# Inverse square roots of 160 norms: a power on GpSimd in place of nine VectorE passes

## The chip, the cores and the metric

The kernel runs on one core of one Trainium2 chip. A core has five engines that each work through their own list of instructions in order and wait for each other by semaphores: TensorE (matrix products; PE in the profile, and PEld for its loads of weights), VectorE (DVE), ScalarE (ACT), GpSimd (POOL) and SyncE (SP, which here only issues DMAs). TensorE writes its results to PSUM; the other data lie in SBUF, over 128 partitions. The metric is the device time of one execution in microseconds (us), as the median of several runs.

## The reference

Eight residual layers are applied in a row to a float32 tensor `x` of shape (2, 1024, 256): two batches of 1024 tokens of 256 channels.

```python
x = x + L0_attn_a(layernorm(x))    # softcapped attention, 16 heads
x = x + L0_ffn(layernorm(x))       # 256 -> 512 -> 512 -> 256, relu
x = x + L0_attn_b(layernorm(x))    # causal attention, 16 heads of 16
x = x + L0_ffn(layernorm(x))
x = x + L1_attn_a(layernorm(x))    # difference of two softmaxes, softmax again, rms norm
x = x + L1_ffn(layernorm(x))       # gated, 256 -> 2048 -> 256, 4-bit weights
x = x + L1_attn_b(layernorm(x))    # a linear model that learns along the tokens
x = x + L1_ffn(layernorm(x))
```

Inverse square roots of a sum plus a small constant appear in three places: in every `layernorm` (eps 1e-5), in the rms norm of each head in `L1_attn_a`, and three times in `L1_attn_b`: keys are divided by their length, the outputs are normalised twice, and the recurrent step itself has one:

```python
def step(S, inp):                                # 64 steps of 16 tokens each
    qi, ki, vi, ei = inp
    kh = einsum('bchd,bhde->bche', ki, S)
    mu = mean(kh, -1); rstd = rsqrt(var(kh, -1) + 1e-6)
    kh_hat = (kh - mu) * rstd
    g = w * kh_hat + b - (vi - ki); gw = g * w
    v_new = (gw - mean(gw) - kh_hat * mean(gw * kh_hat)) * rstd
    ...
    S = S - einsum('bchd,bche->bhde', ki * ei, v_new)
```

Each step needs the `S` of the step before. (The kernel prepares its data so that the mean of `kh` need not be taken off.)

## The kernel before, in words

`x` stays in SBUF as 16 tiles of 128 tokens (`self.x`). The work runs in five functions, with the feed-forward layers woven between the attention work: `attn_a_ffn0` (0 to some 445 us in the profile), `attn_b` (to some 876 us), `ffn0_dequantize` (to 1024 us; it also unpacks the 4-bit weights), `attn_d_ffn1` (to some 2100 us) and `ttt_ffn1` (the linear model and the last feed-forward layer, to the end).

The order of the work is written by hand. `in_order()` (line 372) makes PE, DVE, ACT and POOL execute their instructions in the order in which the Python code emits them; nothing is moved later. Each function cuts its work into small steps and emits them by due times: in `attn_d_ffn1` by the table `SCHED`, in `ttt_ffn1` by the table `TTT`. A round of the linear model is one of the 64 recurrent steps. It emits the tokens `K Q k q d 0 1 s 2 3` in this order, and a step of other work whose due time is `n + m` goes into round `n` at the fraction `m` of that list. `0` is `squares`, `1` is `root`, `s` updates the state, `2` is `gradient`, `3` is `finish` (lines 1984 to 2013). One tile of 128 tokens in both batches is eight rounds.

`rsqrt` (line 260) is called 160 times. It computes `1/sqrt(scale * x + add)` on VectorE in nine instructions (lines 269 to 279): `n` is the scaled sum, the integer form of `n` times -0.5 plus a constant is a first guess, and seven more passes refine it. Its result is the inverse root with a **minus sign**, and the callers are written for that. The calls:

- `layernorm_apply` (line 294), 64 calls, of 128 partitions x 2 columns. `layernorm_stats` finds mean and variance on VectorE and turns the sign of the mean on GpSimd (line 291); `layernorm_apply` takes the inverse root and then normalises the two tiles on GpSimd (line 300). `layernorm_turn` (or `turn` in `ffn0_pieces`) transposes them on TensorE (lines 315, 521) and copies them with a factor -1.
- `root` of a linear-model step (line 1989), 64 calls of 128 x 4. ScalarE squares `kh`, VectorE sums (line 1987), takes the inverse root, and multiplies (`hat`, line 1992).
- `normalize` of the keys (line 1805), 8 calls of 128 x 32, with one more pass that turns the sign (line 1808), and `root` of the outputs (line 2048), 16 calls of 128 x 32: the first (`step` 0) right after its sum (line 2046), the second (`step` 1) one due time later.
- `root` in `attn_d_out` (line 1406), 8 calls of 128 x 32; `normalize` (line 1416) uses the result, for the first three tiles at once, for later tiles about a round later.

GpSimd's other work in `attn_d_ffn1` is `rescale` (lines 1307 to 1315) and `lower` (line 1331), both inside the chain of each pair of heads; in `ttt_ffn1` it has `by_w` (line 1818), `halves` (line 1858, which waits for a DMA) and `gate` (lines 2056, 2059).

Of the kernel before, what the change touches and what calls it, by code (L numbers as in the profile page):

```python
# [10 lines left out]
F32 = mybir.dt.float32  # L11
I32 = mybir.dt.int32
BF16 = mybir.dt.bfloat16
AF = mybir.ActivationFunctionType
ALU = mybir.AluOpType
# [6 lines left out]
P = 128  # L22
# [117 lines left out]
class Net:  # L140
# [17 lines left out]
    def make_constants(self):  # L158
        nc, const = self.nc, self.const
        self.ident = const.tile([P, P], F32, name="ident")  # L160
        make_identity(nc, self.ident)

        self.neg = const.tile([P, P], F32, name="neg")
        nc.gpsimd.memset(self.neg, 0.0)
        nc.gpsimd.affine_select(
            out=self.neg, in_=self.neg, compare_op=ALU.is_ge, fill=NEG, base=0,
            pattern=[[-1, P]], channel_multiplier=1,
        )
        self.tri = const.tile([P, P], F32, name="tri")
        nc.gpsimd.memset(self.tri, 1.0)  # L170
        nc.gpsimd.affine_select(
            out=self.tri, in_=self.tri, compare_op=ALU.is_ge, fill=0.0, base=0,
            pattern=[[1, P]], channel_multiplier=-1,
        )

        self.ident_h, self.neg_h, self.negT_h = (
            const.tile([P, P], BF16, name=n) for n in ("ident_h", "neg_h", "negT_h")
        )
        nc.vector.tensor_copy(self.ident_h, self.ident)
        nc.vector.tensor_copy(self.neg_h, self.neg)  # L180
        nc.vector.tensor_scalar(
            self.negT_h, self.tri, 1.0, -NEG, ALU.subtract, ALU.mult
        )
        self.eps = {}
        for v in (1e-5, 1e-6, 1e-8):
            e = const.tile([P, 1], F32, name=f"eps{len(self.eps)}")
            nc.gpsimd.memset(e, v)
            self.eps[v] = e
        self.minus12 = const.tile([P, 1], F32, name="minus12")
        nc.gpsimd.memset(self.minus12, -12.0)  # L190

# [67 lines left out]

    def rsqrt(self, work, x, scale, add, tag):  # L260

        nc = self.nc
        y, z, w, n = (
            work.tile(list(x.shape), F32, tag=f"{tag}_{k}", name=f"rsq_{k}") for k in "yzwn"
        )
        k = (1024.0 / 27.0) ** 2
        nc.vector.tensor_scalar(n, x, k * scale, k * add, ALU.mult, ALU.add)
        nc.vector.tensor_scalar(  # L270
            y.bitcast(I32), n.bitcast(I32), -0.5, 1597463007.0, ALU.mult, ALU.add
        )
        nc.vector.tensor_tensor(z, y, y, ALU.mult)
        nc.vector.tensor_tensor(w, z, n, ALU.mult)
        nc.vector.scalar_tensor_tensor(z, w, -10.0 / 3.0, w, ALU.add, ALU.mult)
        nc.vector.scalar_tensor_tensor(y, z, 5.0, y, ALU.add, ALU.mult)
        nc.vector.tensor_tensor(z, y, y, ALU.mult)
        nc.vector.tensor_tensor(w, z, n, ALU.mult)
        nc.vector.scalar_tensor_tensor(y, w, -64.0 / 3.0, y, ALU.add, ALU.mult)  # L279
        return y  # L280

    def layernorm_stats(self, work, tiles):
# [26 lines left out]
    def layernorm_turn(self, work, pt, xn, by_parity, on_vector=False, bufs=2):  # L309

        nc = self.nc
        for b in range(B):
            for kc in range(2):
                src = xn[:, b, kc::2] if by_parity else xn[:, b, kc * P : (kc + 1) * P]
                nc.tensor.transpose(pt[:, kc, b * P : (b + 1) * P], src, self.ident)
        xT = work.tile([P, 2, B * P], F32, tag="xT", name="xT", bufs=bufs)
        if on_vector:
            nc.vector.tensor_scalar_mul(xT, pt, -1.0)
        else:
            nc.scalar.activation(xT, pt, AF.Copy, scale=-1.0)  # L320
        return xT

    def project(self, out, xT, tt, w, lo, hi):
# [174 lines left out]
    def ffn0_pieces(self, work, bank, i, w1, w2, w3, b1, b2, b3, scalar=False):  # L498
# [16 lines left out]
        def turn(p):  # L515
            if p == 0:
                f.xT = work.tile([P, 2, 512], F32, tag="fx", name="fxT", bufs=1 + scalar)
            pt = bank("ln_t").rearrange("p (k t) -> p k t", k=2)
            for j in range(2):
                for kc in range(2):  # L520
                    nc.tensor.transpose(
                        pt[:, kc, j * P : (j + 1) * P], f.xn[p][:, j, kc * P : (kc + 1) * P],
                        self.ident,
                    )
            xT = f.xT[:, :, 2 * p * P : 2 * (p + 1) * P]
            if scalar:
                nc.scalar.activation(xT, pt, AF.Copy, scale=-1.0)
            else:
                nc.vector.tensor_scalar_mul(xT, pt, -1.0)

        def hidden(m, part, src, w, bias, dst):
            n = w.shape[1]
# [863 lines left out]
    def attn_d_out(self, ps, work, tile_, wo, i):  # L1396


        nc = self.nc

        def squares():
            flat = tile_.turned.rearrange("p b t n d -> p (b t n) d")
            tile_.sq = work.tile([P, 32, 16], F32, tag="pair", name="sq", bufs=1)
            nc.gpsimd.tensor_tensor(tile_.sq, flat[:, :, 0:16], flat[:, :, 0:16], ALU.mult)

        def root():
            flat = tile_.turned.rearrange("p b t n d -> p (b t n) d")
            r, s2 = (work.tile([P, 32], F32, tag=k, name=k) for k in ("r", "s2"))
            nc.vector.tensor_reduce(r, tile_.sq, AX.X, ALU.add)
            nc.vector.scalar_tensor_tensor(  # L1410
                s2, flat[:, :, 16], 16e-8, flat[:, :, 16], ALU.mult, ALU.mult
            )
            nc.vector.tensor_tensor(r, r, s2, ALU.add)
            tile_.r = self.rsqrt(work, r, 1.0 / 16.0, 0.0, "or")

        def normalize():
            pair = work.tile([P, 4, 4, 32], F32, tag="pair", name="pair", bufs=1)
            by_pair = tile_.turned.rearrange("p b (u t) n d -> p (b u) t n d", t=2)
            rt = tile_.r.rearrange("p (i t n) -> p i t n", t=2, n=4)
            for t in range(2):  # L1420
                nc.vector.tensor_tensor(
                    pair[:, :, :, 16 * t : 16 * t + 16], by_pair[:, :, t, :, 0:16],
                    rt[:, :, t, :].unsqueeze(3).to_broadcast([P, 4, 4, 16]), ALU.mult,
                )
            tile_.yT = work.tile([P, 4, P], F32, tag="yT", name="yT", bufs=1)
            nc.vector.transpose(
                tile_.yT.rearrange("p i q -> p (i q)"), pair.rearrange("p i n d -> p (i n d)")
            )

        def project():  # L1430
            po = self.bank(ps, "po").rearrange("p (b c) -> p b c", b=B)
            for b in range(B):
                for u in range(2):
                    nc.tensor.matmul(
                        po[:, b], tile_.yT[:, 2 * b + u, :], wo[:, u, :],
                        start=(u == 0), stop=(u == 1),
                    )

                xs = self.x[:, b * NB + i, :]
                nc.vector.tensor_tensor(xs, xs, po[:, b], ALU.subtract)  # L1440

        return squares, root, normalize, project

# [113 lines left out]
    def ttt_ffn1(self, w, deq):  # L1557
# [11 lines left out]
        with ExitStack() as ctx:  # L1569
# [33 lines left out]

            t.w2 = big.tile([P, 4, D], F32, name="w2")
            for b in range(B):
                nc.vector.scalar_tensor_tensor(
                    t.w2[:, 2 * b : 2 * b + 2, :], w["ln_w_hc"], -1.0, w["ln_w_hc"],
                    ALU.mult, ALU.mult,
                )

            t.ones = big.tile([1, P], F32, name="ones")
# [3 lines left out]
            for kc in range(2):  # L1615
                wv = w["wqkv"][:, kc, 512:768]
                nc.vector.scalar_tensor_tensor(wv, wv, -1.0, w["ln_w"], ALU.mult, ALU.mult)

                nc.vector.tensor_scalar(
                    w["wo"][:, kc, :], w["wo"][:, kc, :], w["norm_w"][:, kc : kc + 1], -1.0,  # L1620
                    ALU.mult, ALU.mult,
                )
            t.w_out = big.tile([P, C], F32, name="w_out")
            nc.vector.tensor_scalar_mul(t.w_out, w["ln_w"], -1.0)
            t.S = big.tile([P, 4, D], F32, name="S0")
            nc.vector.memset(t.S, 0.0)
            ctx.enter_context(self.in_order())
# [103 lines left out]
    def ttt_inputs(self, i):  # L1731
# [73 lines left out]
        def normalize():  # L1805
            t_.uk = work.tile([P, B, 8, 2, 2, D], F32, tag="uk", name="uk", bufs=1)
            rk = self.rsqrt(work, t_.rk, 1.0, 1e-6, "rk")
            nc.vector.tensor_scalar_mul(rk, rk, -1.0)
            kn = t_.uk[:, :, :, :, 1, :].rearrange("p b h f d -> p (b h f) d")
            nc.vector.tensor_tensor(  # L1810
                kn, t_.k.rearrange("p b (h d) -> p (b h) d", d=D),
# [113 lines left out]
        def own_rates():  # L1925
# [7 lines left out]
            nc.vector.tensor_reduce(  # L1933
                eta.rearrange("p n (b f) -> p f b n", f=2), own, AX.X, ALU.add
            )
            nc.vector.tensor_scalar_add(eta, eta, 1.0)

        def gates():
            sg = t_.sg = work.tile([P, B, C], F32, tag="sg", name="sg")
# [16 lines left out]
    def ttt_step(self, n, data, last):  # L1956
# [25 lines left out]
                )  # L1982

        def squares():
            sq, own.sm = tile_("k_sq"), tile_("var", (P, 4))
            nc.scalar.activation(sq, own.kh, AF.Square)
            nc.vector.tensor_reduce(own.sm, sq, AX.X, ALU.add)

        def root():
            own.rstd = self.rsqrt(work, own.sm, 1.0 / D, 1e-6, "kr")  # L1990
            own.hat = tile_("hat")
            nc.vector.tensor_tensor(own.hat, own.kh, by_g(own.rstd), ALU.mult)

# [23 lines left out]
    def ttt_outputs(self, i, data):  # L2017
# [36 lines left out]
        def gate():  # L2054
            o = data.o
            nc.gpsimd.tensor_tensor(
                o, o, t.w_out.unsqueeze(1).to_broadcast([P, B, C]), ALU.mult
            )
            nc.gpsimd.tensor_tensor(o, o, data.q, ALU.add)

# [240 lines left out]
```

## Time and profile before

| what | value |
|---|---|
| median of 3 runs | 2863.79 us (2859.41 to 2870.02) |
| span of the profiled execution | 2865.0 us, 66910 instructions |
| mean granted TensorE clock | 0.932 |
| ScalarE busy | 1330.0 us (46%) |
| GpSimd busy | 1063.2 us (37%) |
| nine lines of `rsqrt`, VectorE busy in all | 284 us in 1440 instructions |

The profile has one time for the profiled execution, its span: from the first to the last instruction. It lies 1.2 us above the median of the timed runs, inside their range. A line of groups reads: line of the kernel, engine, operation, output <- input by tile names, shapes, count | busy time in all, mean ns of one | idle time of the engine just before them and what ended it. A line of the time view reads: start, duration, engine, line, operation, tiles, count, and in brackets how long the engine had been idle and what it waited for.

### The profile page before, as it was taken

What the parts mean: (1) busy time and instruction counts of PE and PEld (TensorE: products, weight loads), DVE (VectorE), ACT (ScalarE), POOL (GpSimd) and SP (SyncE); (2) the same over time, 40 slices, a digit from 0 to 9 for tenths busy, and PEclk for the clock granted to TensorE, in tenths of its full rate; (3) what the DMA queues carried; (4) which work ended last, traced back from release to release, by engine and by line L of the source; (5) the groups of instructions that cost most, each with busy time, mean ns of one, the idle gap of its engine ahead of it and who ended that gap; (6) DMA issues with size and microseconds to landing.
All of it is one profiled execution on the core that took longest, in us unless ns stands there. A gap on an engine that the chain in (4) does not pass through costs nothing.

```text
span 2865.0 us, 66910 instructions
## 1 busy us (share of the span) xinstructions
PE 2520.3 (88%) x26384; PEld 1555.7 (54%) x26384; DVE 2028.8 (71%) x6762; ACT 1330.0 (46%) x2800; POOL 1063.2 (37%) x1600
## 2 busy tenths in 40 slices
PE   6999998999998877988888888888868999989888
PEld 2334334444433444655655555555646777767777
DVE  5777774766767968679786878788656767767651
ACT  2686870345454435676666675757611222212110
POOL 3444242211115757567554665565510001101000
PEclk9999998999999966999998999899978999999898
DMA  4000000000001100000000000000011110101100
GB/s 122 1 1 1 1 1 1 1 1 1 1 1 45 45 1 1 1 1 1 1 1 1 1 1 1 1 1 1 1 35 25 25 25 22 21 15 35 25 9 15
DMA packets 61978, 35.37 MB, mean 12 GB/s; under 512 B 43216, under 2 KB 58080, under 8 KB 61664
## 3 DMA queue, kind: packets, MB, share of 16 engines
q1 hardware_dynamic: 59472, 29.49, 4.0%
q8 instruction: 207, 3.39, 0.5%
q10 hardware_dynamic: 2192, 1.61, 0.2%
q14 instruction: 107, 0.88, 0.1%
HBM read 22.68 MB, written 8.39 MB: 11 GB/s over the span
## 4 chain that ended last, share of the span: by engine, by line
PE 38%; DVE 14%; POOL 4%; ACT 4%; issue 3%; SPq 1%; DMA 1%; ACTq 0%; POOLq 0%; DVEq 0%
PE ph L1521 6%; PE pg L2115 5%; PE e L1273 4%; DVE p L1284 4%; PE pu L2115 4%; PE po L2133 3%; PE dT L1345 3%; PE po L1540 2%; DVE p L1323 2%; POOL p L1331 1%; PE py L1375 1%; POOL p L1311 1%; ACT p L1294 1%; PE kh L1726 1%; PE pq L327 1%
## 5 line engine op out<-in xcount | busy, mean ns | idle before, releaser
L1294 ACT ACTIVATE p<-p,nm 128x128 f32<-128x128 f32 (+7 forms) x512 | 391.2, 769 | 79.8 <-DVE nm L1290 42.2
L1284 DVE CUSTOM_DVE_ANT_0 p<-e,mask 128x512 f32<-128x512 f32 (+3 forms) x768 | 382.3, 553 | 61.4 <-PE e L1273 61.0
L1331 POOL TENSOR_SCALAR p<-p,md 128x128 f32<-128x128 f32 (+7 forms) x256 | 241.6, 948 | 180.0 <-DVE md L1323 162.6
L1359 ACT ACTIVATE pT<-dT 128x384 f32<-128x384 f32 (+3 forms) x384 | 176.6, 487 | 203.2 <-PE dT L1345 202.2
L1273 PE MATMUL e<-kT,qT 32*128 32x512 f32 (+3 forms) x1536 | 230.5, 580 | 43.7 <-DVE nm L1284 40.8
L1345 PE MATMUL dT<-ident,p 128*128 128x128 f32 x1152 | 197.1, 297 | 65.2 <-POOL p L1331 36.6
L1323 DVE CUSTOM_DVE_ANT_0 p<-p,nrs 128x128 f32<-128x128 f32 (+7 forms) x256 | 221.3, 890 | 25.9 <-POOL p L1315 25.7
L938 ACT ACTIVATE pr<-s 128x512 f32<-128x512 f32 (+3 forms) x384 | 157.3, 496 | 162.9 <-PE s L933 154.2
L1311 POOL TENSOR_SCALAR p<-p,ra,neg_lam 128x128 f32<-128x128 f32 (+7 forms) x256 | 219.5, 857 | 9.2
L1345 PEld LDWEIGHTS dT<-ident,p 128*128 128x128 f32 x1152 | 138.0, 149 | 153.5 <-POOL p L1331 67.9
L654 ACT ACTIVATE pr<-s 128x1024 f32<-128x1024 f32 (+1 forms) x192 | 145.4, 813 | 125.6 <-PE s L648 77.4
L2115 PE MATMUL pg<-xT,gate 128*128 128x256 f32 x576 | 158.6, 423 | 4.6 <-ACT inter L2120 3.4
L898 PE MATMUL s<-kT,qT 32*128 32x512 f32 (+3 forms) x768 | 155.0, 518 | 4.3 <-DVE q_pad L906 2.5
L906 DVE CUSTOM_DVE_ANT_0 masked<-s,mask 128x128 f32<-128x128 f32 (+3 forms) x256 | 110.7, 487 | 59.1 <-PE s L898 59.0
L659 ACT ACTIVATE pr<-pr 128x1024 f32<-128x1024 f32 (+1 forms) x192 | 152.2, 852 | 0.0
L2133 PE MATMUL po<-down,inter 128*128 128x256 f32 x576 | 144.2, 395 | 5.8 <-DVE inter L2125 5.8
L1273 PEld LDWEIGHTS e<-kT,qT 32*128 32x128 f32 x1536 | 84.8, 203 | 116.3 <-DVE nm L1284 72.7
L662 POOL TENSOR_SCALAR_AFFINE_SELECT pr<-pr 128x256 f32<-128x256 f32 x128 | 89.3, 716 | 152.1 <-ACT pr L659 55.1
L2115 PE MATMUL pu<-xT,up 128*128 128x256 f32 x576 | 141.3, 389 | 0.8 <-ACT inter L2120 0.7
L2120 ACT ACTIVATE inter<-pg 128x512 f32<-128x512 f32 x72 | 43.0, 597 | 195.7 <-PE pg L2115 195.7
L2115 PEld LDWEIGHTS pg<-xT,gate 128*128 128x128 f32 x576 | 116.5, 209 | 27.1 <-issue 4.7
L300 POOL TENSOR_SCALAR ln_xn<-x,ln_mv,rsq_y 128x256 f32<-128x256 f32 x128 | 89.8, 710 | 108.1 <-DVE rsq_y L279 88.8
(295 smaller groups left out, 5344.1 us busy)
## 6 DMA issues: line engine op xcount, KB each, us to landing
uk_d<-uk SPq DMA_DIRECT2D x128, 32.0 KB, 1.9
r<-uk_d SPq DMA_DIRECT2D x8, 512.0 KB, 3.5
x<-in_L_attn_a_X SPq DMA_DIRECT2D x4, 512.0 KB, 6.7
qh_d<-qh SPq DMA_DIRECT2D x8, 256.0 KB, 2.1
o<-qh_d SPq DMA_DIRECT2D x128, 16.0 KB, 1.8
out<-x SPq DMA_DIRECT2D x4, 512.0 KB, 4.4
w<-in_L_ffn_W2T SPq DMA_DIRECT2D x1, 1024.0 KB, 7.7
pk<-in_L_ffn_gate_packed SPq DMA_DIRECT2D x8, 128.0 KB, 2.4
```

The costliest lines, as they stand in the source:

```text
L938: nc.scalar.activation(pr[:, g, off:512], tiles[g][:, 0:m], AF.Exp, scale=0.25)
L1273: nc.tensor.matmul(own.tiles[h][:, a, 0 : hi - lo], made["q"][r : r + 32, a, t, :], kT[r : r + 32, a, lo:hi], start=True, stop=True,)
L1284: nc.vector.tensor_tensor_reduce(own.p[h][a][:, lo:hi], own.tiles[h][:, a, 0 : hi - lo], neg_row[:, T - nk + lo : T - nk + hi], -1.0, 3e38 ...
L1294: nc.scalar.activation(own.p[h][a], own.p[h][a], AF.Exp, bias=own.nm[:, h, a : a + 1], scale=-1.0, accum_out=own.sm[:, h, a : a + 1],)
L1311: nc.gpsimd.tensor_scalar(p1, p1, own.ra[:, h : h + 1], nlam[:, head : head + 1], ALU.mult, ALU.mult)
L1323: nc.vector.tensor_tensor_reduce(p0, p0, p1, own.nrs[:, h : h + 1], 3e38, ALU.add, ALU.min, own.md[:, h : h + 1],)
L1331: nc.gpsimd.tensor_scalar(p0, p0, -1.0, own.md[:, h : h + 1], ALU.mult, ALU.add)
L1345: nc.tensor.transpose(dT[:, n, :], own.p[h][0][:, kb * P : (kb + 1) * P], self.ident)
L1359: nc.scalar.activation(shared[t, s + h][:, lo:hi, :], own.dT[h, part][:, 0 : hi - lo, :], AF.Exp)
L1521: nc.tensor.matmul(ph[:, j, :], w[:, kc, m * P : (m + 1) * P], f.xT[:, kc, :], start=(kc == 0), stop=(kc == 1),)
L2115: nc.tensor.matmul(ph[:, j, :], m_[:, kc, m * P : (m + 1) * P], f.xT[:, kc, :], start=(kc == 0), stop=(kc == 1),)
L2133: nc.tensor.matmul(f.po[:, b], inter[m // 2][:, m % 2, b * P : (b + 1) * P], wd[:, m % 2, (m // 2) * C : (m // 2 + 1) * C], start=(b == m ...
```

## The change

`rsqrt` becomes one or two GpSimd instructions. If a scale is given, the first computes `scale * x + add`; the second raises that to the power -0.5, the exponent being a constant column that is read for every element. The result is positive now, so every caller's sign changes: copies lose their factor -1, two products lose theirs, the pass of line 1808 and the tile `w_out` go, and `eta` gets a factor -1 in the instruction that adds its constant.

In the recurrent step both numbers of the first instruction are moved elsewhere: ScalarE squares with scale `D ** -0.5`, so that the sum is a mean, and the tile of the squares has a 17th column that is set to 1e-6 once and is summed along. There, `rsqrt` is a single GpSimd instruction.

```diff
+        self.root = const.tile([P, 1], F32, name="root")
+        nc.gpsimd.memset(self.root, -0.5)
...
     def rsqrt(self, work, x, scale, add, tag):
         nc = self.nc
-        y, z, w, n = (
-            work.tile(list(x.shape), F32, tag=f"{tag}_{k}", name=f"rsq_{k}") for k in "yzwn"
-        )
-        k = (1024.0 / 27.0) ** 2
-        nc.vector.tensor_scalar(n, x, k * scale, k * add, ALU.mult, ALU.add)
-        nc.vector.tensor_scalar(
-            y.bitcast(I32), n.bitcast(I32), -0.5, 1597463007.0, ALU.mult, ALU.add
-        )
-        nc.vector.tensor_tensor(z, y, y, ALU.mult)
-        nc.vector.tensor_tensor(w, z, n, ALU.mult)
-        nc.vector.scalar_tensor_tensor(z, w, -10.0 / 3.0, w, ALU.add, ALU.mult)
-        nc.vector.scalar_tensor_tensor(y, z, 5.0, y, ALU.add, ALU.mult)
-        nc.vector.tensor_tensor(z, y, y, ALU.mult)
-        nc.vector.tensor_tensor(w, z, n, ALU.mult)
-        nc.vector.scalar_tensor_tensor(y, w, -64.0 / 3.0, y, ALU.add, ALU.mult)
+        y = work.tile(list(x.shape), F32, tag=f"{tag}_y", name="rsq_y")
+        if scale is not None:
+            n = work.tile(list(x.shape), F32, tag=f"{tag}_n", name="rsq_n")
+            nc.gpsimd.tensor_scalar(n, x, scale, add, ALU.mult, ALU.add)
+            x = n
+        nc.gpsimd.tensor_tensor(y, x, self.root.to_broadcast(list(x.shape)), ALU.pow)
         return y
...
-            nc.vector.tensor_scalar_mul(xT, pt, -1.0)
+            nc.vector.tensor_copy(xT, pt)
         else:
-            nc.scalar.activation(xT, pt, AF.Copy, scale=-1.0)
+            nc.scalar.copy(xT, pt)
...
-                nc.vector.tensor_tensor(xs, xs, po[:, b], ALU.subtract)
+                nc.vector.tensor_tensor(xs, xs, po[:, b], ALU.add)
...
-            t.w_out = big.tile([P, C], F32, name="w_out")
-            nc.vector.tensor_scalar_mul(t.w_out, w["ln_w"], -1.0)
+            t.sq = [big.tile([P, 4, D + 1], F32, name=f"k_sq{j}") for j in range(2)]
+            for sq in t.sq:
+                nc.gpsimd.memset(sq, 1e-6)
...
             rk = self.rsqrt(work, t_.rk, 1.0, 1e-6, "rk")
-            nc.vector.tensor_scalar_mul(rk, rk, -1.0)
...
-            nc.vector.tensor_scalar_add(eta, eta, 1.0)
+            nc.vector.tensor_scalar(eta, eta, -1.0, -1.0, ALU.mult, ALU.add)
...
         def squares():
-            sq, own.sm = tile_("k_sq"), tile_("var", (P, 4))
-            nc.scalar.activation(sq, own.kh, AF.Square)
+            sq, own.sm = t.sq[n % 2], tile_("var", (P, 4))
+            nc.scalar.activation(sq[:, :, 0:D], own.kh, AF.Square, scale=D ** -0.5)
             nc.vector.tensor_reduce(own.sm, sq, AX.X, ALU.add)
 
         def root():
-            own.rstd = self.rsqrt(work, own.sm, 1.0 / D, 1e-6, "kr")
+            own.rstd = self.rsqrt(work, own.sm, None, None, "kr")
```

More of the change, by code (lines that the diff above doesn't have):

```diff
@@ L526, in turn @@
             if scalar:
-                nc.scalar.activation(xT, pt, AF.Copy, scale=-1.0)
+                nc.scalar.copy(xT, pt)
             else:
-                nc.vector.tensor_scalar_mul(xT, pt, -1.0)
+                nc.vector.tensor_copy(xT, pt)
         def hidden(m, part, src, w, bias, dst):
@@ L1605, in ttt_ffn1 @@
             for b in range(B):
-                nc.vector.scalar_tensor_tensor(
-                    t.w2[:, 2 * b : 2 * b + 2, :], w["ln_w_hc"], -1.0, w["ln_w_hc"],
-                    ALU.mult, ALU.mult,
+                nc.vector.tensor_tensor(
+                    t.w2[:, 2 * b : 2 * b + 2, :], w["ln_w_hc"], w["ln_w_hc"], ALU.mult
                 )
@@ L1617, in ttt_ffn1 @@
                 nc.vector.scalar_tensor_tensor(wv, wv, -1.0, w["ln_w"], ALU.mult, ALU.mult)
-                nc.vector.tensor_scalar(
-                    w["wo"][:, kc, :], w["wo"][:, kc, :], w["norm_w"][:, kc : kc + 1], -1.0,
-                    ALU.mult, ALU.mult,
-                )
-            t.w_out = big.tile([P, C], F32, name="w_out")
-            nc.vector.tensor_scalar_mul(t.w_out, w["ln_w"], -1.0)
+                nc.vector.tensor_scalar_mul(
+                    w["wo"][:, kc, :], w["wo"][:, kc, :], w["norm_w"][:, kc : kc + 1]
+                )
+            t.sq = [big.tile([P, 4, D + 1], F32, name=f"k_sq{j}") for j in range(2)]
+            for sq in t.sq:
+                nc.gpsimd.memset(sq, 1e-6)
             t.S = big.tile([P, 4, D], F32, name="S0")
@@ L2056, in gate @@
             nc.gpsimd.tensor_tensor(
-                o, o, t.w_out.unsqueeze(1).to_broadcast([P, B, C]), ALU.mult
+                o, o, t.w["ln_w"].unsqueeze(1).to_broadcast([P, B, C]), ALU.mult
             )
```

## The prediction

> **What bounds the kernel now.** I read the page's first two parts, then the waits around the tile that all inverse roots write, then the time view of one recurrent step and one layer norm, then TensorE's waits and the chain of waits by stage.
>
> ```profile
> span 2865.0 us, 66910 instructions
> ...
> PE 2520.3 (88%) x26384; PEld 1555.7 (54%) x26384; DVE 2028.8 (71%) x6762; ACT 1330.0 (46%) x2800; POOL 1063.2 (37%) x1600
> ...
> PE   6999998999998877988888888888868999989888
> ...
> DVE  5777774766767968679786878788656767767651
> ...
> POOL 3444242211115757567554665565510001101000
> ```
>
> TensorE bounds the whole: 88% busy, 345 us idle. So an edit on VectorE or GpSimd pays only where TensorE waits for it. Three regions differ. To 1020 us TensorE is full except where it waits for a layer norm. In the attention of 1100 to 2100 us it is 847 of 1000 us busy, and VectorE (782) and GpSimd (591) take turns in its chain. In the linear model (2126 to 2760 us) it is busy 578 of 634 us, and GpSimd is nearly empty (59 us).
>
> The waits around the inverse roots (us, times):
>
> ```profile
>   POOL ln_xn L300: 88.8, 46
> ...
>   PE ln_t L315: 43.2, 12
> ...
>   PE ln_t L521: 26.0, 9
> ```
>
> GpSimd already waits for the nine passes before it normalises, and TensorE waits for that. One layer norm at 880 us:
>
> ```profile
> 880.30 0.18 DVE L289 BATCH_NORM_AGGREGATE ln_mv<-ln_st 128x2 f32<-128x6 f32 x1
> ...
> 880.67 0.19 POOL L291 TENSOR_SCALAR ln_mv<-ln_mv 128x2 f32<-128x2 f32 x1 [7.91 <-DVE ln_mv L289]
> ...
> 882.43 1.10 POOL L300 TENSOR_SCALAR ln_xn<-x,ln_mv,rsq_y 128x256 f32<-128x256 f32 x2 [1.57 <-DVE rsq_y L279]
> ```
>
> The variance is there at 880.48; GpSimd starts its small operation 0.1 to 0.2 us later, and then idles 1.57 us for VectorE. From variance to use: 1.95 us.
>
> One recurrent step, and what TensorE waits for in the linear model (total, times, longest):
>
> ```profile
> 2405.47 0.22 DVE L1987 TENSOR_REDUCE var<-k_sq 128x4 f32<-128x64 f32 x1 [0.23 <-ACT k_sq L1986]
> ...
> 2405.73 0.17 DVE L269 TENSOR_SCALAR rsq_n<-var 128x4 f32<-128x4 f32 x1
> 2405.93 0.17 DVE L270 TENSOR_SCALAR rsq_y<-rsq_n 128x4 int32<-128x4 int32 x1
> ...
> 2407.32 0.16 DVE L279 SCALAR_TENSOR_TENSOR rsq_y<-rsq_w,rsq_y 128x4 f32<-128x4 f32 x1
> 2407.58 0.23 DVE L1992 TENSOR_TENSOR hat<-kh,rsq_y 128x64 f32<-128x64 f32 x1
> ```
>
> ```profile
> PE kh L1726 <- DVE vs L2013: 6.8, 13, 1.9
> PE po L2133 <- DVE inter L2125: 5.8, 3, 3.0
> PE pqk L327 <- ACT xT L320: 4.8, 7, 0.7
> ...
> PE kh L1726 <- DVE hat L1992: 3.2, 1, 3.2
> PE kh L1726 <- DVE S L1703: 3.1, 4, 2.0
> ```
>
> Sum to product take 1.89 us of nine dependent passes, one each 0.2 us. The waits that VectorE (or a norm, through xT) causes add up to 23.7 us; most of the other 32 us are "issue". That is the ceiling here, whatever VectorE gains.
>
> **The price of a power.** No row of the trace shows it. Low end: an ordinary small GpSimd operation, 0.19 us (the sign of the mean, 128x2) for 2 or 4 columns, 0.27 us for 32 (the sign row plus 32 columns of 2.5 ns, from 1272 ns for 512 columns of line 2056). High end: every column as dear as such a whole instruction, 0.19 us each after a start of 0.19: 0.57, 0.95 and 6.3 us for 2, 4 and 32 columns. Between them I take the row of the same function: VectorE needs nine passes; nine passes at GpSimd's 2.5 ns a column are 22 ns, and a general power is a logarithm, a product and an exponential, so three times that, 65 ns a column (an estimate): 0.32, 0.45 and 2.3 us. The hand-overs have rows: 0.1 us from VectorE to GpSimd (the mean's sign after its sum, three instances looked at) and 0.05 us back (VectorE's line 1323 after GpSimd's line 1315).
>
> The row of GpSimd's two-input multiply (1272 ns, line 2056) against VectorE's of the same size (692 ns, line 2052) is 1.84 to 1. The Trainium skill, GPSIMD Engine Reference, section Engine selection, speaks against the change with just this: elementwise work belongs on VectorE, GpSimd being about twice as slow. By it alone one power would still cost only two of the nine passes it replaces, and the time would be that of the low end, 2788. The same page, section Instruction dispatch, says that the first call of a freshly loaded GpSimd routine costs about 6 us more; no row here shows it, and by it the sum below would be 6 us higher, once.
>
> **Layer norms (64 calls).** Out: nine passes. In: two GpSimd operations behind the mean's sign, which ran beside the passes before and is now in series: 0.1 + 0.19 + 0.19 + 0.32 + gaps 0.05 = 0.85 us instead of 1.95, so 1.1 us earlier. Before 1100 us TensorE waits 14 times for a norm (53.8 us in all). At 455 us GpSimd is held by memsets until 454.1, so that nothing is won there and 0.5 us lost; elsewhere about 1 us: **-10 us**. The later norms are counted with their stages.
>
> **Attention, 1100 to 2100 us (14 norms and 8 head norms).** Out: 45 us of VectorE and 6 us of gaps. Of these, 36 us stand in the chain of waits. The next chain is close behind (TensorE also waits 35 us for GpSimd's `lower` and 22 for ScalarE), so I take half: -18. In: 14 x 0.51 + 8 x 2.5 = 27 us on GpSimd, queued ahead of `rescale` and `lower`; GpSimd is in the chain for 89 of its 591 busy us, 15%: +4. New wait: for the first three tiles the product follows the root at once, so VectorE, and `highest` and `difference` behind it, wait 0.9 us longer each: +3. Sum **-11 us**.
>
> **Linear model.** Each of the 64 steps: 0.1 + 0.45 + 0.05 = 0.6 us instead of 1.89, 1.3 earlier, with an empty GpSimd queue ahead of it. The keys' norm (2.2 us of passes inside the last part of a step, 7 times in the chain) vanishes from VectorE's list: its sum is ready 7 us before the product, and GpSimd runs ahead. The second output norm likewise (3.4 us ahead). The first output norm follows its sum at once: 2.66 us instead of 2.21, but the step's own root then runs beside the product instead of after it, with passes that took 1.1 us beside `gate`. `gate` collides with `gradient` instead, so I count that as even. Of the ceiling of 23.7 us I take two thirds, since the waits that remain end on PSUM, DMA or ScalarE next: **-16 us**. If nothing were hidden by TensorE's own work, it would be 64 x 1.3.
>
> **Tail and the rest.** One norm in the open at 2809 us: **-1**. At nothing: the copies without a factor (ScalarE 587 ns against 596, VectorE 677 against 686), 17 columns summed instead of 16 (220 ns for 64 elements, so 14 ns for 4 at most), `eta`'s two factors in one pass, and two memsets against `w_out`'s pass, both ahead of the first step, where GpSimd and VectorE wait for the first keys; in the open they would cost 0.2 us each.
>
> Sum: -10 - 11 - 16 - 1 = -38, from the span 2865.0 to **2827**; the median shown lies 1.2 lower, so **2826**.
>
> **Rivals.**
> - **All of it counts.** At the low price GpSimd's load is small; 36 + 1 in the attention, 24 in the model, 14 x 1.1 at the norms, 1: 2788. For it: the chain of waits holds 85 us of the passes from 1020 us on. Against: the ceilings above.
> - **Hidden anyway.** TensorE is the bound, its order is fixed by hand, and the passes leave behind idle VectorE. Only the norms pay: 2865 - 10 = 2855. For it: in two steps of the time view (2405 and 2416 us), `vs` was ready 3 us before TensorE came to it.
> - **Slower: powers of 32 columns.** VectorE's list is in order, so it stands still at the first output norm until GpSimd is done, with the next root, `S` and the step's end behind it; in the attention `rescale` stands behind the power. At the high price (6.3 us): norms -8, steps -10, first output norm 8 x 2, second 8 x 1.3 (it no longer fits into its 3.4 us), attention -18 + 9 + 15, tail -1: about +13, 2878. From there, every us more costs 8 + 8 + 7 + 4 = 27. At 8 us it is 2925. It decides from about 6.4 us for 32 columns.
>
> **Chances.** Forecast (2805 to 2849) 0.45; all counts 0.10; hidden, or a price near 6 us, 0.23; slower 0.22. A measurement can tell some 0.5% from no change: faster 0.55, same 0.23, slower 0.22. The range runs from the low end, 2788, past the high end's 2878 to 2890; above it I leave out 0.15, below 0.04.
>
> **What will show it.** The duration and the start-to-start distance of the power's rows by shape: 0.3, 0.45, 2.3 us. `hat` some 0.6 us after `var`; `ln_xn` 0.85 us after its variance; VectorE's busy time down by about 285 us. In the linear model the waits of kh for `vs`, `hat`, `S` should fall to about a third. The forecast is wrong if `hat` waits over 1.9 us for GpSimd, if `o` (line 2052) waits over 6 us, or if the wait of dT for `lower` grows from 35 us by more than 10.

## The result and the profile after

The changed kernel takes 2889.7 us (median of four runs, 2885.9 to 2896.5) against 2861.6 us for the kernel before: a ratio of 1.0091 (95% interval 1.0069 to 1.0113). It is slower by 0.9%, where 2826 us, 1.4% faster, had been forecast. The profiled execution has a span of 2894.3 us, 29.3 us above the one of before.

The first two parts of the page after:

```profile
span 2894.3 us, 65730 instructions
...
PE 2530.2 (87%) x26384; PEld 1562.5 (54%) x26384; DVE 1774.7 (61%) x5313; ACT 1328.6 (46%) x2800; POOL 1355.8 (47%) x1859
...
DVE  4777663866757856777677878787533544444421
...
POOL 4445332312117767667565767575432434444320
```

VectorE has 254 us less work, as the change meant. But GpSimd has 293 us more. TensorE has the same 26384 matmuls; its idle time grew by 19 us and its busy time by 10. The groups of the power's line, with shapes apart (count, busy time in us, mean in ns):

```profile
L270 POOL TENSOR_TENSOR rsq_y<-rsq_n,root 128x32 f32<-128x32 f32 x32 | 174.1, 5442 | 2.7
...
L270 POOL TENSOR_TENSOR rsq_y<-var,root 128x4 f32<-128x4 f32 x64 | 64.7, 1011 | 246.4 <-DVE var L1976 246.4
L270 POOL TENSOR_TENSOR rsq_y<-rsq_n,root 128x2 f32<-128x2 f32 x64 | 51.3, 802 | 5.2
```

These are the rows that the trace of before could not have: 5.4 us for 32 columns, 1.01 for 4, and 0.70 (the shortest of the 64) for 2. The forecast had 2.3, 0.45 and 0.32. The waits of VectorE for the power (total us, times, longest):

```profile
DVE hat L1981 <- POOL rsq_y L270: 74.5, 64, 8.8
DVE o L2041 <- POOL rsq_y L270: 62.3, 16, 5.8
DVE pair L1412 <- POOL rsq_y L270: 23.8, 4, 6.3
DVE uk L1799 <- POOL rsq_y L270: 21.8, 8, 5.9
```

The first row is the largest and looks like the culprit; it is not. `hat` waits about 1.13 us in most steps, a wait that replaces 1.89 us of passes. `o`, `pair` and `uk` stand behind a power of 32 columns. The time view after, at the first output norm of a tile (start, duration):

```profile
2467.52 0.22 DVE L1976 TENSOR_REDUCE var<-k_sq 128x4 f32<-128x68 f32 x1
2467.66 0.68 DVE L2035 TENSOR_REDUCE o_r<-o_sq 128x32 f32<-128x512 f32 x1
...
2468.73 5.41 POOL L270 TENSOR_TENSOR rsq_y<-rsq_n,root 128x32 f32<-128x32 f32 x1
2474.10 1.01 POOL L270 TENSOR_TENSOR rsq_y<-var,root 128x4 f32<-128x4 f32 x1
2474.17 0.69 DVE L2041 TENSOR_TENSOR o<-o,rsq_y 128x512 f32<-128x512 f32 x1 [5.84 <-POOL rsq_y L270]
...
2475.15 0.23 DVE L1981 TENSOR_TENSOR hat<-kh,rsq_y 128x64 f32<-128x64 f32 x1 [0.28 <-POOL rsq_y L270]
...
2476.43 1.27 POOL L2048 TENSOR_TENSOR o<-o,q 128x512 f32<-128x512 f32 x1
2476.47 1.31 DVE L1989 TENSOR_TENSOR gp<-gp,r 128x64 f32<-128x64 f32 x1
```

The step's sum was ready at 2467.74, but its root stands in GpSimd's list behind the long power, and `hat` starts 7.4 us after the sum, where most other steps have 1.1 to 1.2. The bracket at `hat` shows only the last 0.28 us of this. The same step in the profile of before:

```profile
2451.77 0.22 DVE L1987 TENSOR_REDUCE var<-k_sq 128x4 f32<-128x64 f32 x1
...
2454.81 0.69 DVE L2052 TENSOR_TENSOR o<-o,rsq_y 128x512 f32<-128x512 f32 x1 [0.21 <-DVE rsq_y L279]
...
2455.82 1.11 DVE L273 TENSOR_TENSOR rsq_z<-rsq_y 128x4 f32<-128x4 f32 x1
...
2459.18 0.23 DVE L1992 TENSOR_TENSOR hat<-kh,rsq_y 128x64 f32<-128x64 f32 x1
```

There, too, `hat` came 7.2 us after the sum: nine passes for `o`, then nine for the step, two of which took 1.1 us beside `gate`. In this step the wait for `o` (3.6 us longer from the sum) uses up what the change gains between `o` and `hat` (3.4 us shorter). And as `o` is later, `gate` now runs beside `gradient`, whose lines 1988 and 1989 take 0.42 and 1.31 us instead of 0.22 and 0.23. The step is 1.5 us longer, of which 0.2 come before `hat` and 1.3 from `gate`. TensorE pays further on:

```profile
PE kh L1716 <- DVE vs L2002: 15.5, 10, 3.9
...
PE po L2122 <- DVE inter L2114: 11.7, 5, 3.9
...
PE pu L2104 <- DVE inter L2114: 7.1, 1, 7.1
```

Before, these waits were 6.8, 5.8 and 0 us. Where the time came from, by stage, in the profiled executions (the attention ends with the start of the last `e` matmul, the steps begin and end with `var`; "keys" is the start of the linear model between them). The start stage of kernels with equal code there differs by up to 7 us, so single cells are read to some 4 us. The kernels with names are those of the experiments.

| us | to first `e` | attention | keys | 64 steps | rest | span |
|---|---|---|---|---|---|---|
| before | 1040.7 | 1013.7 | 72.0 | 625.5 | 113.1 | 2865.0 |
| after | 1028.1 | 1020.9 | 80.8 | 650.1 | 114.4 | 2894.3 |
| no_wide | 1027.0 | 1009.4 | 76.6 | 620.9 | 111.5 | 2845.4 |
| only_wide | 1040.3 | 1024.2 | 81.0 | 662.8 | 114.0 | 2922.3 |
| cheap_wide | 1025.2 | 999.1 | 69.7 | 611.9 | 110.6 | 2816.5 |
| moved | 1032.1 | 1009.4 | 79.7 | 614.3 | 111.8 | 2847.3 |

TensorE's idle time in the same stages (the stage less TensorE's busy time) is steadier from kernel to kernel. The last column is the clock granted to TensorE in the steps, as a share of full speed:

| us idle | to first `e` | attention | keys | 64 steps | clock in the steps |
|---|---|---|---|---|---|
| before | 104.3 | 152.9 | 17.2 | 53.3 | 0.94 |
| after | 91.9 | 162.1 | 22.7 | 67.9 | 0.92 |
| no_wide | 93.0 | 150.1 | 17.2 | 49.9 | 0.94 |
| only_wide | 103.5 | 166.5 | 23.1 | 70.7 | 0.90 |
| model_wide | 94.5 | 150.1 | 22.0 | 66.7 | 0.93 |
| cheap_wide | 93.1 | 147.7 | 15.8 | 52.1 | 0.96 |
| moved | 93.1 | 150.2 | 21.1 | 49.9 | 0.95 |

Of the 24.6 us that the steps lost, 14.7 are idle time. The other 9.9 are busy time: the same matmuls took 582.2 us instead of 572.3, at a granted clock of 0.92 instead of 0.94. Why the clock was lower is not shown.

### The profile page after: what moved, and what is told of

It reads as the page before. It is cut to its first block, busy times and chain, and to the rows that moved or that the text cites. A ratio compares the mean times of both kernels' runs of the same rounds, so it can differ in the third digit from the quotient of the medians.

```text
span 2894.3 us, 65730 instructions
## 1 busy us (share of the span) xinstructions
PE 2530.2 (87%) x26384; PEld 1562.5 (54%) x26384; DVE 1774.7 (61%) x5313; ACT 1328.6 (46%) x2800; POOL 1355.8 (47%) x1859
## 4 chain that ended last, share of the span: by engine, by line
PE 36%; DVE 11%; POOL 10%; ACT 3%; issue 3%; SPq 1%; DMA 1%; POOLq 0%; DVEq 0%; ACTq 0%
PE ph L1512 5%; PE pg L2104 4%; PE po L2122 4%; POOL rsq_y L270 4%; DVE p L1275 4%; PE pu L2104 4%; PE e L1264 3%; PE dT L1336 3%; DVE p L1314 2%; POOL p L1302 2%; PE po L1531 2%; POOL p L1322 2%; PE kh L1716 1%; PE pq L318 1%; PE pqk L318 1%
## 5 line engine op out<-in xcount | busy, mean ns | idle before, releaser
L1336 PE MATMUL dT<-ident,p 128*128 128x128 f32 x1152 | 199.2, 300 | 75.6 <-POOL p L1322 47.3
L270 POOL TENSOR_TENSOR rsq_y<-rsq_n,root 128x2 f32<-128x2 f32 (+1 forms) x96 | 225.5, 2348 | 7.9
L270 POOL TENSOR_TENSOR rsq_y<-var,root 128x4 f32<-128x4 f32 x64 | 64.7, 1011 | 246.4 <-DVE var L1976 246.4
L933 POOL TENSOR_SCALAR_AFFINE_SELECT pr<-pr 128x512 f32<-128x512 f32 x64 | 40.6, 635 | 226.5 <-ACT pr L929 226.5
```

What stands on the lines that cost most here:

```text
L270: nc.gpsimd.tensor_tensor(y, x, self.root.to_broadcast(list(x.shape)), ALU.pow)
L1336: nc.tensor.transpose(dT[:, n, :], own.p[h][0][:, kb * P : (kb + 1) * P], self.ident)
```

## The experiments

My theory was now that the price of the 32-column power, with VectorE standing in order behind it, makes the whole loss. It had two rivals: that the hand-over between the engines in each of the 64 steps makes it, or that GpSimd work of any price upsets the order. All experiments start from the changed kernel. Some use `rsqrt_dve`: the old nine passes with a sign turned in the last two, so that the result is positive and no caller changes.

```diff
+        nc.vector.scalar_tensor_tensor(w, z, -1.0, n, ALU.mult, ALU.mult)
+        nc.vector.scalar_tensor_tensor(y, w, 64.0 / 3.0, y, ALU.add, ALU.mult)
```

### The change in three parts

Four kernels choose for each call between the power and the passes; no_wide is this, the others alike:

```diff
-            tile_.r = self.rsqrt(work, r, 1.0 / 16.0, 0.0, "or")
+            tile_.r = self.rsqrt_dve(work, r, 1.0 / 16.0, 0.0, "or")
...
-            rk = self.rsqrt(work, t_.rk, 1.0, 1e-6, "rk")
+            rk = self.rsqrt_dve(work, t_.rk, 1.0, 1e-6, "rk")
...
-            r = self.rsqrt(work, data.o_r, 1.0 / D, (1e-6, 4e-6)[step], "rk")
+            r = self.rsqrt_dve(work, data.o_r, 1.0 / D, (1e-6, 4e-6)[step], "rk")
```

no_wide:

> The change with the 32 roots of 32 columns taken back to nine VectorE passes (written so that the result is positive); the powers of 2 and 4 columns stay. Theory (the price of the 32-column power, 5.4 us on GpSimd with VectorE standing still behind it, makes the loss; the powers of 2 and 4 columns gain): faster than before by 13 to 30 us, ratio 0.990 to 0.995, and the linear model's 64 steps shorter than before's 634 us. Rival 1 (the hand-over in every recurrent step costs, since the time to the use of the root is short but VectorE idles 74.5 us for it): slower than before, 1.002 to 1.008. Rival 2 (any work moved to GpSimd upsets an order that was tuned for VectorE, whatever its price): within 0.4% of before or slower, with the attention of 1100 to 2100 us still longer.

only_wide:

> The change for the roots of 32 columns alone (8 of the keys, 16 of the outputs, 8 of the head norms); the layer norms and the recurrent step keep nine VectorE passes. Theory: slower than before by more than the whole change, since the gains of the other two are missing: 26 + 13 (norms) + 5 to 15 (steps) = 44 to 54 us, ratio 1.014 to 1.020. Rival 1 (the step): at most +12 us, 1.000 to 1.004. Rival 2 (order): about a third of the whole loss, 1.002 to 1.006.

only_norms:

> The change for the 64 layer norms alone (2 columns); all other roots keep nine VectorE passes. The changed kernel reached 1040 us of before 12 us earlier, with norms alone in that part. Theory: 10 to 16 us faster, ratio 0.994 to 0.9965, almost all of it before the attention of 1100 us; there the norms are even. Rival 2 (order): the 12 us are won, and 5 to 10 of them lost again in the attention, where GpSimd's queue holds the power ahead of its own work: 0.997 to 1.000.

only_steps:

> The change for the recurrent step alone (4 columns, one power of 1.01 us, with the mean's factor in ScalarE's square and the constant as a 17th column); all other roots keep nine VectorE passes. From the sum to the product the changed kernel takes 1.2 us where before takes 1.89. Theory: 3 to 15 us faster, ratio 0.995 to 0.999; TensorE's own work hides part of 64 x 0.7 = 45 us. Rival 1 (the step's hand-over costs): slower by 15 us or more, 1.005 or above. Rival 2 (order): within 3 us of before or slower.

Measured, as ratios to before: no_wide 0.9898 (0.9878 to 0.9918), only_wide 1.0199 (1.0179 to 1.0219), only_norms 0.9948 (0.9929 to 0.9968), only_steps 0.9957 (0.9940 to 0.9973). The parts add up: -0.52, -0.43 and +1.99% make +1.04%, and the change has +0.91%. The measured ratios lie in the theory's ranges, or within 0.0002 of them. Both rivals fall: the steps alone gain, although `hat` waits just as long in no_wide (74.7 us) as after, and the norms alone gain. The powers of 2 and 4 columns earn 1%, those of 32 columns lose 2%.

### The price without the place

cheap_wide keeps the order and makes the wide power a product, which leaves the 32 wide roots out of the computation:

```diff
+            if x.shape[-1] == 32:
+                scale, add = 0.0, 1.0
             nc.gpsimd.tensor_scalar(n, x, scale, add, ALU.mult, ALU.add)
             x = n
-        nc.gpsimd.tensor_tensor(y, x, self.root.to_broadcast(list(x.shape)), ALU.pow)
+        op = ALU.mult if x.shape[-1] == 32 else ALU.pow
+        nc.gpsimd.tensor_tensor(y, x, self.root.to_broadcast(list(x.shape)), op)
```

> The changed kernel with the order of all instructions kept, but the 32 powers of 32 columns replaced by a product of the same tiles (the operation before it then writes a constant 1, so that keys, outputs and head norms are scaled by a fixed number and not normalised: that part of the computation is left out). The GpSimd instruction should take about 0.25 us in place of 5.4; hand-overs, queue and order stay. Theory (the price of the wide power makes the loss): at least as fast as the kernel that keeps the wide roots on VectorE (0.990 of before), since 32 x 9 passes are gone for little: ratio 0.980 to 0.990. Rival (taking the wide roots off VectorE hurts at any price, by hand-over and by its place in GpSimd's queue): 0.995 or above.

Measured: 0.9844 (0.9818 to 0.9869), 2822 us. The place in the order does no harm at a low price. Against the change, only the duration of 32 instructions differs, and the values that they write; the difference is 2.5%. That the values matter little is likely, since moved and passes_model (below), which compute everything, have 614 to 615 us in the steps, against 612 here and 650 after. Of VectorE's waits, this is left:

```profile
DVE o L2065 <- POOL rsq_y L273: 5.3, 8, 0.7
```

### The place without the price

In model_wide, only the first of the three edits of no_wide is made, so the linear model keeps its wide powers in line; moved changes their place as well:

```diff
-        0.71, 1.04, 1.918, 1.923, 2.086, 2.518, 2.955, 2.923, 3.183, 3.82, 4.025, 2.963,
+        0.71, 1.04, 1.918, 1.923, 2.086, 2.518, 2.955, 2.923, 3.183, 3.71, 4.12, 4.125, 2.963,
...
-    "outputs": (0.58, 0.585, 1.55, 1.555, 1.66, 2.086, 2.6, 2.7, 2.958, 3.69, 4.43, 4.786),
+    "outputs": (
+        0.58, 0.585, 1.55, 1.71, 2.12, 2.125, 2.55, 2.6, 2.7, 2.71, 3.2, 3.69,
+        4.43, 4.786,
+    ),
...
-                t_.q = work.tile([P, B, C], F32, tag="q", name="q")
+                t_.q = work.tile([P, B, C], F32, tag="q", name="q", bufs=3)
...
+        def power(step):
+            data.o_r = self.rsqrt(work, data.o_r, 1.0 / D, (1e-6, 4e-6)[step], "rk")
+
         def root(step):
-            r = self.rsqrt(work, data.o_r, 1.0 / D, (1e-6, 4e-6)[step], "rk")
+            r = data.o_r
```

The keys' `normalize` is split in the same way, and each `power` is a step of its own in the lists; to make room, the sum is scaled in its own tile.

> The changed kernel with the 8 head norms of the attention taken back to nine VectorE passes; the 24 wide powers of the linear model stay where the change put them. By the landmarks of the runs so far the wide powers cost 8 to 10 us in the attention, about 8 at the linear model's start and 25 to 37 in its steps. Theory: 8 to 14 us below the changed kernel, ratio to before 1.003 to 1.007. Rival (the head norms in the attention, where GpSimd is itself in the chain, make most of the loss): 0.995 or below.

> As the last, with the 24 wide powers of the linear model at the same price but at another place: each is issued on GpSimd right behind a recurrent step's own power, and its product on VectorE about half a round later, so that neither VectorE nor a step's power should stand behind it (gate, open, by_w and the second sum follow, and the tile q has a third buffer for that). Theory A (it is VectorE standing still in order behind the power that costs): 0.985 to 0.992, like the kernel with wide roots on VectorE or a little faster, and idle time of VectorE before o and uk under a third of 80 us. Theory B (5.4 us of GpSimd cost wherever they are placed, by holding its later work): no better than the last, 1.000 or above.

Measured: model_wide 1.0067 (1.0046 to 1.0088), moved 0.9930 (0.9908 to 0.9951). The same 24 powers at the same 5.4 us cost 1.4% less where VectorE has other work in the meantime. Theory B falls; theory A's range is missed by 0.001. moved is no better than no_wide, though, and VectorE still stands:

```profile
DVE o L2070 <- POOL rsq_y L273: 21.3, 9, 5.3
DVE uk L1826 <- POOL rsq_y L273: 15.0, 8, 5.9
```

That is 36 us where 27 or less was expected, against 84 after. The ratio of model_wide is 0.0024, or 7 us, below that of the change, with intervals that overlap, so the times alone do not show the attention's share of the loss. TensorE's idle time in the attention does: 162 us after and 167 in only_wide, with the head norms as powers, against 150 in no_wide and model_wide and 153 before. The eight head norms cost some 12 to 14 us of idle time there. The rival, that they make most of the loss, falls, since model_wide is still slower than before.

Which steps lose is seen in the mean time from one step's sum (`var`) to the next, over steps 8 to 55, by the step's place in its tile:

| us | 0 | 1 | 2 | 3 | 4 | 5 | 6 | 7 | sum |
|---|---|---|---|---|---|---|---|---|---|
| before | 8.75 | 8.66 | 12.11 | 12.03 | 11.16 | 9.97 | 10.58 | 8.20 | 81.5 |
| only_wide | 8.99 | 9.09 | 15.94 | 14.05 | 10.56 | 9.95 | 10.54 | 7.87 | 87.0 |
| after | 8.60 | 9.11 | 13.54 | 13.32 | 10.71 | 9.64 | 10.75 | 8.84 | 84.5 |
| moved | 8.69 | 8.83 | 11.23 | 12.34 | 10.59 | 9.35 | 10.57 | 8.83 | 80.4 |
| cheap_wide | 8.75 | 8.52 | 11.06 | 12.18 | 10.49 | 9.46 | 10.48 | 8.83 | 79.8 |

Interval 2 holds the first output norm, 3 the second, 4 the keys. The loss sits in 2 and 3, where the root is in line with the step; at the keys it is nil, as the wait for the power there (1.5 us or less in five of these six tiles of the change) is shorter than the ten passes that it replaced (2.2 us).

### The price by itself, and a price in the middle

The kernel price adds a row of powers at the start of no_wide:

> The kernel with the wide roots on VectorE, and at its start a row of powers on GpSimd that nothing reads: 1, 2, 4, 8, 16, 32, 64, 128 columns of 128 partitions, twice; then 33 columns of small numbers, 34 with exponent 2, 35 with exponent 0.3, 36 columns of only 32 partitions, 37 as a product, 39 again as the plain power. Its time says nothing. From 0.70, 1.01 and 5.41 us for 2, 4 and 32 columns: 0.38 us and 157 ns a column, so 0.54, 0.70, 1.01, 1.64, 2.9, 5.4, 10.4, 20.5 us. If the price is that of the function, exponent and values change nothing; 0.3 against 2 differing would speak for a loop that depends on the exponent. If the first power of the program pays for loading code, it is about 6 us longer than its second instance.

Lines of GpSimd's time view there:

```profile
2.70 0.57 POOL L2178 TENSOR_TENSOR py<-px,root 128x1 f32<-128x1 f32 x1
...
12.15 2.90 POOL L2178 TENSOR_TENSOR py<-px,root 128x16 f32<-128x16 f32 x1
...
32.66 20.73 POOL L2178 TENSOR_TENSOR py<-px,root 128x128 f32<-128x128 f32 x1
...
109.60 5.95 POOL L2187 TENSOR_TENSOR py<-px,pexp 128x35 f32<-128x35 f32 x1
115.63 6.10 POOL L2190 TENSOR_TENSOR py<-px,root 32x36 f32<-32x36 f32 x1
121.81 0.27 POOL L2193 TENSOR_TENSOR py<-px 128x37 f32<-128x37 f32 x1
```

From 16 to 128 columns the slope is (20.73 - 2.90) / 112 = 159 ns a column, with some 0.36 us of start. In the repeat of the row, the starts agree with the durations: 10.60 us from the power of 64 columns to the next one, and 20.80 from that of 128. The exponents and values tried and the number of partitions change nothing; a product of 37 columns takes 0.27 us. The first power of the program took 0.57 us, right behind the memset ahead of it; the second instance of its shape took 0.55.

passes_all writes the root as twelve small GpSimd instructions (`rsqrt_gp`: the nine passes, of which the three that take two tensors and a number are split in two) in place of the wide power; passes_model does so in the linear model and uses `rsqrt_dve` in the attention.

```diff
+        g.tensor_scalar(n, x, k * scale, k * add, ALU.mult, ALU.add)
+        g.tensor_scalar(
+            y.bitcast(I32), n.bitcast(I32), -0.5, 1597463007.0, ALU.mult, ALU.add
+        )
+        g.tensor_tensor(z, y, y, ALU.mult)
+        g.tensor_tensor(z, z, n, ALU.mult)
+        g.tensor_scalar(x, z, 1.0, -10.0 / 3.0, ALU.mult, ALU.add)
+        g.tensor_tensor(z, z, x, ALU.mult)
...
```

> The changed kernel with the 32 wide powers replaced by the nine passes written as twelve small GpSimd instructions (integer guess, products, sums) in the same place of the order; powers of 2 and 4 columns stay, and everything is computed. By 0.19 to 0.27 us each, the root should take about 2.6 to 3.2 us on GpSimd in place of 5.6: a price in the middle. Measured ends: 0.9844 of before with 0.25 us, 1.0091 with 5.4 us. If the loss grows with the price in a straight line, 2.9 us gives 0.997. If most of it comes only once the cover (GpSimd running ahead, VectorE idle anyway) is used up, 0.988 to 0.993. If passes on GpSimd also hold up VectorE, which the power does not (VectorE instructions that ran during a power took no longer), above 0.998.

> As the last, with the 8 head norms of the attention on VectorE in nine passes; only the 24 wide roots of the linear model are twelve passes on GpSimd. It tells whether a root that leaves VectorE in the linear model pays at a middle price: the kernel with all wide roots on VectorE is at 0.990. Straight line: 0.996 to 0.999 (5.4 us gave 1.0067). Cover first: 0.987 to 0.992.

Measured: passes_all 0.9923 (0.9900 to 0.9947), passes_model 0.9926 (0.9906 to 0.9946). The twelve took 3.7 us, more than expected. From the end of the first output norm's sum to `o` it is now 3.9 us, where cheap_wide has 0.7 and the change 5.8. A straight line between those two ends would give 1.000 at 3.9 us; the measured value and its interval lie below. From 0.7 to 3.9 us each us costs about 7 us in all, from 3.9 to 5.8 about 25. So part of the price is covered; with three prices, where the cover ends is not shown. passes_model is no faster than no_wide (0.9898, and the intervals overlap), so it is not shown that a wide root gains by leaving VectorE at this price.

## Why the prediction was wrong, point by point

- **The step that failed is "The price of a power".** It took 65 ns a column; the runs show 159, so 5.4 us for 32 columns instead of 2.3. The high end that the prediction itself set, 0.19 us a column, was the close one. The stated range, 2788 to 2890, was drawn wide enough for it and just holds 2889.7; the value taken, and with it the way the time would move, was wrong.
- **The other terms at a low price.** cheap_wide has 2822 us where the forecast was 2826, and by stage, against before, -15.5 before the attention (forecast -10), -14.6 in it (-11), -13.6 in the steps (-16). The sizes agree, the mechanism only in part. TensorE's idle time fell by 11.2, 5.2 and 1.2 us; the rest is shorter busy time, in the steps 559.9 us at a granted clock of 0.96 instead of 572.3 at 0.94, for which the prediction had no term. The waits of `kh` for `vs`, `hat` and `S`, which were to fall to a third of their 13.1 us, were 13.5. So the agreement in the steps is luck.
- **Layer norms.** -12.6 us to the first `e` against -10: the size was right, though the price was off by two and the path was another. In the time view after, at 874 us, GpSimd's three small operations take 1.35 us from the first's start to `ln_xn`; with 0.1 us of hand-over that is 1.45 us from variance to use, against 1.95 before and 0.85 worked out. TensorE's waits for the norms in this stage, which were to give the 10 us, are 50.9 us after and were 51.9 before. What shrank are waits for other work: for `xT` at line 327 (now 318) from 7.7 to 3.3 us, for `h` from 7.6 to 4.8, for `pr` of GpSimd from 6.3 to 3.8. VectorE is busy 53 us less in this stage; that this is the reason was not tested.
- **Attention -11.** Measured +7. TensorE's wait for `lower` grew from 36.6 to 47.3 us, past the bound of 10 that the prediction had set as its own refutation. The product stood behind the root in four tiles, not three, and VectorE waited 23.8 us for it (`pair`). Without the wide powers the stage has 1009 us (no_wide and model_wide).
- **Linear model -16.** +25 in the steps and some 9 at the keys ahead of them (5.5 of these are idle time of TensorE). The time from a step's sum to its product did shorten, but to 1.2 us where 0.6 was expected. The first output norm, counted as even, lengthens its interval by 1.4 us a tile, and the second, counted as covered by 3.4 us, by 1.3. At the first, the prediction had named both sides, the step's passes gone from behind `o` and `gate` on `gradient` instead, and set them as even at 2.3 us for the power. At 5.4 us the wait for `o` takes the gain (`hat` 7.2 us after the sum before, 7.4 after), and the collision, 1.3 us, stays. Against no_wide, where `hat` comes 3.4 us after the sum, the wide power costs 2.6 us there.
- **The keys' norm "vanishes".** It did not: its power is emitted behind the step's own power and waits there, and `uk` stands 21.8 us in all (8.3 in only_wide, where the step has no power). In the loop this costs nothing that can be seen, since the interval of the keys did not grow.
- **The slower rival** names the mechanism that the runs confirm: VectorE in line at the output norms, with the next root behind it. Its size was off: 2878 us at 6.3 us, when 5.4 us already gave 2890. It counted nothing at the keys ahead of the first step. By its own sum it is even with before at a power of 5.8 us (6.3 less 13 / 27). By the straight line between passes_all and the change, the ratio is 1 at 4.8 us from sum to product, which for a single power, with the 0.4 us around it, is an estimated 4.4 us. Its slope of 27 us for each us is near the 25 between those two kernels.
- **The marks.** `o` never waited over 6 us (5.84), though the loss was there: that bound was set from the wrong point of decision. `hat` waited longer than 1.9 us in two steps, and the longer of these waits, 8.8 us, stands in no_wide too (8.7): this mark says nothing of the wide power. VectorE's busy time fell by 254 us and not by 285, as its other instructions took some 20 us longer, about 9 of them in `gp`.

The fastest kernel that computes everything is no_wide, with powers of 2 and 4 columns and the wide roots on VectorE: 2840 us, 1% below before and 2% below the change. moved, passes_all and passes_model lie within 0.4% of it, with intervals that overlap.

## What to carry to other kernels

Price a replaced operation by its width in every place where it stands: one and the same edit gained at 2 and 4 columns and lost at 32, and the sum hid both. Where an unknown price has bounds far apart, and the product stands in line behind it, take the dearer bound or make the change only where it is narrow. A wait that is the largest in the list can be a gain, if what it replaced was longer; compare it with the same place in the kernel before, and not with the other steps. The interval from one step to the next shows what counts.

## What the runs showed of the hardware

A power on GpSimd costs 159 ns a column for the three exponents tried and for 32 as for 128 partitions, some 60 times the 2.5 ns of its multiply (1272 ns for 512 columns).

While a power runs, VectorE's instructions with two SBUF inputs take no longer, 0.23 us here, as before:

```profile
2486.14 5.41 POOL L270 TENSOR_TENSOR rsq_y<-rsq_n,root 128x32 f32<-128x32 f32 x1
2486.27 0.23 DVE L1990 TENSOR_TENSOR gp<-gp,hat 128x64 f32<-128x64 f32 x1
```

Beside the ordinary product of `gate`, such an instruction takes 1.31 us instead of 0.23: line 1989 in the time view of the section on the result starts 0.04 us after line 2048 and ends 0.08 us after it. The Trainium skill, SBUF — State Buffer, section Who interferes with whom, says that a VectorE instruction with two SBUF inputs contends with a GpSimd instruction that reads SBUF, and calls the shared ports an exclusive lock. The rows at `gate` agree; the power reads SBUF too, and its rows do not. Why is not shown.

The Trainium skill, GPSIMD Engine Reference, section Instruction dispatch, which the prediction weighed, gives about 6 us more for the first call of a freshly loaded routine. No run shows it for the power: in the kernel price its first instance took 0.57 us and followed the instruction before it without a gap.
